# A self-attention residual added in DRAM by accumulating transfers instead of on GpSimd

## The chip, the cores and the metric

The kernel runs on one core of one Trainium2 chip. The metric is the device time of that core in microseconds (us), the median of several executions. Everything is float32.

## The reference, cut to what matters

A transformer block works on eight images of 512 rows and 512 features. A cross-attention with modulated layer norm (phase x), a self-attention (phase a), a second cross-attention (phase c) and an MLP (phase m) follow each other, and each adds its result to x:

```python
x = x_q + (out @ Wp + bp)                  # phase x
attn_out = attn_out @ W_proj + b_proj
x = x + gate_a[:, None] * attn_out         # phase a: the line that the change is about
x = x + c_attn_out                         # phase c
x = x + gate_m[:, None] * h                # phase m
```

`gate_a` is a row of 512 numbers for each image. The softmax of phase a runs over 16 heads of 512 x 512 scores.

## The kernel before, in words

**Where x lies.** x travels through DRAM between the phases. Phase x leaves it in `xa` (one tensor for each image), phase a writes `xc`, and phases c and m read `xc`. Phases x and c already add their results by accumulating transfers: GpSimd (POOL) issues a DMA from the SBUF tile `res` to DRAM with `accum_op=ALU.add` (L665). Such a transfer reads the SBUF source and the DRAM destination and writes the sum back. In phase x, `xa` is filled with a copy of x first (L866). Phase c adds in place to `xc`.

**Phase a, `self_phase`.** The work is cut into 32 groups, four for each image `b`, counted `fc` = 0 to 3; a group is four heads. All engines' orders are written out by hand in one loop over the groups (`manual_schedule(engines=None)`): the order in the source is the order on each engine, and an instruction that waits holds up what follows it on its engine. In the turn of group `g`:

- TensorE (PE) makes the transposed scores of the *next* group, four key tiles of 128 (`nxt.scores(k)`, L991). ScalarE (ACT) copies them to `e` in SBUF (L1009) and VectorE (DVE) keeps a running maximum `mx` (L1011).
- `maxima` and `spread` turn the maxima into one negated number for each query (L1022 to L1035), and SyncE (SP) writes these 8 KB to the DRAM row `mxd` (L1040).
- `shift(k)`, L1045: POOL issues eight accumulating DMAs, two for each key tile, which read `mxd` broadcast over the 128 partitions and add it into the `e` tiles in SBUF, 512 KB each. All eight wait for `mxd` to have landed.
- `exp(k)`, L1054: ACT takes the exponential of each shifted tile. POOL and DVE add the tiles up for the denominators (`add_up`, L1061), and PE multiplies with the values (`outputs`, L1071).

The loop calls `g.exp(0)`, `nxt.scores(3)`, `g.exp(1)`, later `g.exp(2)`, and in the next turn `prev.exp(3)`. So a late shift of key tile 0 holds up ACT's copies of the next group's last scores, and with them the maxima of the next group.

**Beside the attention** each turn runs other products, as generators that `pump` advances: values, queries and keys of the coming image in `fc` 0, 2 and 3, and the output projection of the *previous* image, `project(b - 1, t)`, for `t` = 0 and 1 in `fc` 1 and `t` = 2 and 3 in `fc` 2. In `fc` 2 the next image is transposed (L912) and the one after it is loaded, 1 MB on ACT's queue (`load_x`, L900).

**The residual of phase a.** Four steps for each of the 32 tiles of 128 rows:

- `load_tile`, L906: SP loads the tile's rows of x from `xa` into `xr`, four tiles at a time, at the start of `fc` 0. For the last image the loads stand in the tail behind the loop.
- L960: DVE takes the projection out of PSUM and adds the bias row, into `tmp` (tile `res`).
- `add`, L963 and L964: POOL multiplies `tmp` with the gate row and adds it to `xr`.
- `store`, L967: SP writes `xr` to `xc`.

`add` and `store` are put into two lists and run by `flush(0)` and `flush(1)` at two places of the turn: after the shifts were issued, and before `g.exp(0)`. With this placement one tile's `add` and `store` run in the middle of `fc` 1, one early in `fc` 2, and two in the middle of `fc` 2. For the last image, whose projection stands in the tail, they run tile by tile, and phase c begins behind them.

**Queues.** SP's DMAs run on the queue that the profile calls q1, ACT's on q10, and all of POOL's on q0. As the program is built, POOL's DMAs take eight completion semaphores in turn, so that each waits, at its issue, for the POOL DMA eight places before it.

Of the kernel before, what the change touches and what calls it, by code (L numbers as in the profile page):

```python
# [11 lines left out]
F32 = mybir.dt.float32  # L12
I32 = mybir.dt.int32
AF = mybir.ActivationFunctionType
ALU = mybir.AluOpType
# [4 lines left out]
P = 128  # L20
H = 512
KC = H // P
# [7 lines left out]
def tile_pixart_block(ctx: ExitStack, tc: tile.TileContext, a: dict, out: bass.AP):  # L30
    nc = tc.nc
    x, ctx_in, cond = a["x"], a["ctx_1024"], a["cond_1024"]
    B, N, _ = x.shape
    S = ctx_in.shape[1]
    NT = N // P
# [8 lines left out]
    dram = ctx.enter_context(tc.tile_pool(name="dram", bufs=1, space=bass.MemoryType.DRAM))  # L44
# [40 lines left out]
    def bias_cols(name, n=1, at=0):  # L85
        c = col_at[name] + at
        return bcol[:, c : c + n]
# [33 lines left out]
    def load_context(pool):  # L121
# [11 lines left out]
    x_src = {  # L133
        "x": [x[b] for b in range(B)],
        "a": [dram.tile([N, H], F32, name=f"xa_{b}") for b in range(B)],
        "c": [dram.tile([N, H], F32, name=f"xc_{b}") for b in range(B)],
    }
    x_src["m"] = x_src["c"]
    x_dst = {"x": x_src["a"], "a": x_src["c"], "c": x_src["m"], "m": [out[b] for b in range(B)]}
    x_order = [(ph, b) for ph in "xacm" for b in range(B if ph in "xc" else 1)]  # L140
    x_sb = {}
# [11 lines left out]
    with tc.tile_pool(name="setup_ps", bufs=2, space=PSUM) as spp:  # L153
# [4 lines left out]
        for name, n in col_names:  # L158
            at = col_at[name]
            nc.gpsimd.dma_start(  # L160
                out=brow[at : at + n, :],
                in_=a[name][0 : n * P].rearrange("(c p) -> c p", p=P),
# [149 lines left out]
    def fold_value_bias(name, at, w, row, pool, psp, bufs=2):  # L312


        wide = pool.tile([P, KC, P], F32, tag="res", bufs=bufs, name=f"wide_{name}")
        nc.vector.tensor_copy(wide, bias_cols(name, KC, at).unsqueeze(2).to_broadcast([P, KC, P]))
        ps = psp.tile([P, H], F32, tag="m", name=f"fold_ps_{name}")
        for k in range(KC):
            nc.tensor.matmul(
                ps, lhsT=wide[:, k, :], rhs=w[:, k, :], start=(k == 0), stop=(k == KC - 1)  # L320
            )
        nc.vector.tensor_tensor(row, ps, row, ALU.add)
# [16 lines left out]
    with tc.tile_pool(name="ps_s", bufs=2, space=PSUM, reuse_waits="tile") as ps_s:  # L339
# [539 lines left out]
        def self_phase(w, bo_row, work, work_2, ctx_c):  # L879
# [1 line left out]


            w_v, w_q, w_k, w_o = w
            st = [dict(xT=[], v={}, o=[], q={}, k={}, x={}) for _ in range(B)]
            bias = "L1_xcond_b_qkv"
            SQ = 32
            KQ = N // SQ
# [11 lines left out]
            def load_x(b):  # L899
                nc.scalar.dma_start(  # L900
                    out=x_cur, in_=x_src["a"][b].rearrange("(t p) d -> p t d", p=P)
                )

            def load_tile(b, t, queue=nc.scalar):
                xr = work.tile([P, H], F32, tag="xr", bufs=4, name=f"xr_a{b}_{t}")
                queue.dma_start(out=xr, in_=x_src["a"][b][ts(t, P), :])  # L906
                st[b]["x"][t] = xr

            def transpose_x(b, k):
                pt = ps_m.tile([P, H], F32, tag="m", name=f"lnT_ps_a{b}_{k}")  # L910
# [41 lines left out]
            def project(b, t):  # L952
                if t == 0 and b + 1 < B:
                    st[b]["g"] = gate_rows(gate_a, b, work, "a")
                pr = ps_m.tile([P, H], F32, tag="m", name=f"proj_ps_a{b}_{t}")
                for i, _ in enumerate(mm_N(pr, w_o, st[b]["o"], ts(t, P))):
                    if i == KC - 1:
                        xr = st[b]["x"].pop(t)
                        tmp = work.tile([P, H], F32, tag="res", bufs=3, name=f"res_a{b}_{t}")
                        nc.vector.tensor_tensor(tmp, pr, bo_row, ALU.add)  # L960

                        def add():
                            nc.gpsimd.tensor_tensor(tmp, tmp, st[b]["g"], ALU.mult)  # L963
                            nc.gpsimd.tensor_tensor(xr, xr, tmp, ALU.add)  # L964

                        def store():
                            nc.sync.dma_start(out=x_dst["a"][b][ts(t, P), :], in_=xr)  # L967

                        later[0].append(add)
                        later[1].append(store)  # L970
                    yield
# [142 lines left out]
            for k in range(KC):  # L1114
                transpose_x(0, k)
            load_x(1)
            fold_value_bias(bias, 2 * KC, w_o, bo_row, work, ps_m, 3)
            run(queries(0, 0))
            run(keys(0, 0))
            for k, gen in enumerate([values(0, 0), values(0, 1), queries(0, 1), keys(0, 1)]):  # L1120
# [7 lines left out]
            for n, g in enumerate(groups[:-1]):  # L1128
                b, fc = g.b, g.fc
                nxt = groups[n + 1]  # L1130
                more = b + 1 < B
                f = beside(b, fc)
                turning = fc == 2 and more
                if fc == 3:
                    ln = normalise_x("a", b + 2, True) if b + 2 < B else iter(())
                if not more and fc == 1:
                    ctx_c.w_k = load_w("L1_xcond_W_kvc", 0)
                if prev is not None:
                    prev.outputs(1)
                nxt.scores(0)  # L1140
                g.spread()
                if past is not None:
                    past.total()
                    past.finish()
                if prev is not None:
                    prev.add_up(2, [0])
                g.shift(0)
                if prev is not None:
                    prev.add_up(2, [1])
                    prev.exp(3, [0])  # L1150
                for k in range(1, NT):
                    g.shift(k)
                flush(0)
                flush(1)
                if fc == 0 and b > 0:
                    for t in range(NT):
                        load_tile(b - 1, t, nc.sync)
                if fc == 1 and more:
                    next(ln)
                pump(f[0], 4)  # L1160
                nxt.scores(1)
                if fc == 3 or (b, fc) == (0, 0):
                    next(ln, None)
                    next(ln, None)
                elif fc == 0 and more:
                    next(ln)
                if turning:
                    transpose_x(b + 1, 0)
                if prev is not None:
                    prev.exp(3, [1])  # L1170
                    prev.outputs(2)
                if fc == 1 and more:
                    next(ln)
                pump(f[1], 4)
                if fc == 1 and not more:
                    ctx_c.load()
                    ln = ctx_c.norm()
                if turning:
                    transpose_x(b + 1, 1)
                nxt.scores(2)  # L1180
                if turning:
                    transpose_x(b + 1, 2)
                if fc == 2 and not more:
                    next(ln)
                    next(ln)
                if prev is not None:
                    prev.add_up(3)
                if (b, fc) == (0, 0):
                    next(ln)
                if prev is not None:  # L1190
                    prev.outputs(3)
                if turning:
                    transpose_x(b + 1, 3)
                    if b + 2 < B:
                        load_x(b + 2)
                flush(0)
                flush(1)
                g.exp(0)
                pump(f[2], 2)
                nxt.scores(3)  # L1200
                pump(f[2], 2)
                g.exp(1)
                g.add_up(1)
                if fc == 2 and not more:
                    run(ln)
                nxt.maxima()
                g.outputs(0)
                pump(f[3], 4)
                if fc == 2 and not more:
                    ctx_c.transpose()  # L1210
                g.exp(2)
                past, prev = prev, g
# [29 lines left out]
            for k in range(NT):  # L1242
                g.exp(k)
                if k:
                    g.add_up(k)
                g.outputs(k)
                if k == 0:
                    st[g.b]["g"] = gate_rows(gate_a, g.b, work, "a")
                    for t in range(NT):
                        load_tile(B - 1, t, nc.sync)  # L1250
                if k < len(fills):
                    run(fills[k])
            w_c = [load_w("L1_xcond_W_qc", 0, queue=nc.scalar)]
# [59 lines left out]
        with ExitStack() as stack:  # L1313
            ps_m = stack.enter_context(tc.tile_pool(name="ps_x", bufs=2, space=PSUM, reuse_waits="tile"))
# [17 lines left out]
        with tc.tile_pool(name="work_a", bufs=2, reuse_waits="tile") as work, tc.tile_pool(  # L1332
            name="ps_a", bufs=2, space=PSUM, reuse_waits="tile"
        ) as ps_m, tc.tile_pool(
            name="ps_o", bufs=2, space=PSUM, reuse_waits="tile"
# [5 lines left out]
        with ExitStack() as stack:  # L1341
            ps_m = stack.enter_context(
                tc.tile_pool(name="ps_c", bufs=2, space=PSUM, reuse_waits="tile")
            )
# [21 lines left out]
    bo_row = load_row("L1_xcond_b_mlp2", 0, "bo")  # L1366
    with tc.tile_pool(name="mlp", bufs=1, reuse_waits="tile") as mlp, tc.tile_pool(
        name="mlp_w", bufs=MC // KC - 1, reuse_waits="tile"
    ) as mlp_w, tc.tile_pool(
        name="ps_q", bufs=6, space=PSUM, reuse_waits="tile"  # L1370
    ) as ps_q, tc.tile_pool(
        name="ps_t", bufs=2, space=PSUM, reuse_waits="tile"
# [10 lines left out]
        xT = xpool.tile([P, KC, N], F32, tag="x", name="xT_m")  # L1383
# [253 lines left out]
```

## Time and profile before

| | us |
|---|---|
| median of 3 runs (2554.19 to 2556.33) | 2554.23 |
| the profiled execution, its own time | 2556.85 |
| its span, first to last instruction | 2555.1 |

| engine | busy us | share |
|---|---|---|
| PE | 2437.6 | 95% |
| DVE | 1776.1 | 70% |
| ACT | 1224.9 | 48% |
| POOL | 1103.1 | 43% |

The page cuts the span into 40 slices of 64 us; a digit is the busy share in tenths.

```profile
PE   7999999989999999999988999998999999999998
...
POOL 2245452277776877768663445445102102012011
PEclk9899999999999999999999999999999999999999
DMA  7323323499999899999995213133111011011010
```

Phase a fills the slices from about 460 us to 1370 us. In it PE stands at 9 or 8, and so does the mean of the 16 DMA engines; after it the DMA engines fall to 0 to 5. The clock granted to PE is full almost everywhere.

These are the transfers that the change touches, as the page's last part lists them: destination, source, queue, count, size of one, and the median time from issue to landing.

```profile
e_a<-mxd_a POOLq DMA_DIRECT2D x256, 512.0 KB, 11.7
xa<-res_x POOLq DMA_DIRECT2D x32, 256.0 KB, 5.2
xr_a<-xa SPq DMA_DIRECT2D x32, 256.0 KB, 6.1
xc<-xr_a SPq DMA_DIRECT2D x32, 256.0 KB, 8.6
```

### The profile page before, as it was taken

The page shows a single profiled execution, that of the slowest core. Times are in us where ns is not written, and L with a number is a line of the kernel's source. Part 1 is how long each engine was busy: PE and PEld are TensorE (multiplying, and loading weights), DVE is VectorE, ACT ScalarE, POOL GpSimd, SP SyncE. Part 2 cuts the span into 40 slices and gives each one's busy share as a digit, 9 for nine tenths or more (in the row PEclk, how much of TensorE's full clock was granted, in tenths as well). Part 3 has the DMA queues.
Part 4 walks back from the last instruction along what each step waited for, and adds up shares of the span by engine and source line. Part 5 has one row for each costly group of instructions (what it writes and reads, how often), then busy time and mean ns, then how long its engine had stood idle before and what let it go on. Part 6 is the DMA issues. An engine that isn't in the chain of part 4 may idle for free. (4 is left out here: it accounts for less than half of the span.)

```text
span 2555.1 us, 35387 instructions
## 1 busy us (share of the span) xinstructions
PE 2437.6 (95%) x13205; PEld 1562.6 (61%) x13205; DVE 1776.1 (70%) x3230; ACT 1224.9 (48%) x2083; POOL 1103.1 (43%) x982
## 2 busy tenths in 40 slices
PE   7999999989999999999988999998999999999998
PEld 3577776323333333333325777777888888888887
DVE  3588886478788888887756888887546545555553
ACT  1466665477676776767643666662121121121220
POOL 2245452277776877768663445445102102012011
PEclk9899999999999999999999999999999999999999
DMA  7323323499999899999995213133111011011010
GB/s 259 135 51 95 89 27 74 102 180 193 198 179 205 183 199 195 180 199 180 216 210 171 72 34 67 18 64 98 36 35 38 33 39 38 25 34 49 20 35 25
DMA packets 116676, 273.44 MB, mean 107 GB/s; under 512 B 12722, under 2 KB 29186, under 8 KB 116378
## 3 DMA queue, kind: packets, MB, share of 16 engines
q0 software_dynamic: 46368, 151.06, 33.0%
q1 hardware_dynamic: 64197, 108.37, 12.6%
q10 hardware_dynamic: 5941, 11.76, 1.3%
q8 instruction: 104, 1.70, 0.3%
q14 instruction: 66, 0.54, 0.1%
HBM read 234.78 MB, written 44.76 MB: 109 GB/s over the span
## 5 line engine op out<-in xcount | busy, mean ns | idle before, releaser
L1546 POOL TENSOR_TENSOR res_m<-res_m,gate_m 128x256 f32<-128x256 f32 x64 | 52.1, 814 | 665.1 <-DVE res_m L1544 665.1
L1045 POOL DMA_DIRECT2D e_a<-mxd_a x256 | 250.4, 2060 | 157.9 <-DMA mxd_a<-mxT_a 148.6
L1054 ACT ACTIVATE e_a<-e_a 128x1024 f32<-128x1024 f32 x256 | 265.1, 1058 | 98.4 <-DMA e_a<-mxd_a 98.0
L1009 ACT COPY e_a<-sT_a 128x1024 f32<-128x1024 f32 x256 | 254.2, 1010 | 91.0 <-DVE mx_a L1011 49.0
L1480 ACT ACTIVATE hT<-hT,bcol 128x512 f32<-128x512 f32 x128 | 91.9, 721 | 237.0 <-DVE hT L1455 228.9
L1061 POOL TENSOR_TENSOR sum_a<-e_a,e_a 128x1024 f32<-128x1024 f32 x64 | 150.2, 2363 | 105.8 <-ACT e_a L1054 105.4
L1011 DVE TENSOR_TENSOR mx_a<-sT_a,mx_a 128x1024 f32<-128x1024 f32 x128 | 150.9, 1216 | 33.6 <-PE sT_a L991 27.9
L1061 POOL TENSOR_TENSOR sum_a<-sum_a,e_a 128x1024 f32<-128x1024 f32 x64 | 171.2, 2686 | 5.3 <-ACT e_a L1054 5.3
L991 PE MATMUL sT_a<-qT_a,kT_a 32*128 32x512 f32 x1024 | 151.4, 640 | 17.7 <-ACT e_a L1009 16.1
L1071 PE MATMUL o_ps_a<-e_a,v 128*32 128x512 f32 x1024 | 152.9, 608 | 12.8 <-ACT e_a L1054 12.8
L1447 PE MATMUL q_ps_h<-x_m,w_L_xcond_W_mlp 128*128 128x256 f32 x512 | 132.3, 381 | 0.0
L1447 PE MATMUL q_ps_h<-xT_m,w_L_xcond_W_mlp 128*128 128x256 f32 x512 | 131.6, 380 | 0.0
L294 PE MATMUL q_ps_a<-xnT_a,w_L_xcond_W_qkv 128*128 128x512 f32 x256 | 124.1, 613 | 7.6 <-ACT xnT_a L914 7.6
L1089 DVE RECIPROCAL rz_a<-z_ps_a 128x512 f32<-128x512 f32 x32 | 107.4, 3357 | 31.9 <-PE z_ps_a L1082 31.9
L1447 PE MATMUL q_ps_h<-x_m,w_s 128*128 128x256 f32 x512 | 121.9, 381 | 5.3 <-DVE w_s L1401 4.6
L302 PE MATMUL proj_ps_a<-w_L_xcond_W_proj,oT_a 128*128 128x512 f32 x256 | 118.1, 605 | 3.1 <-DVE res_a L960 1.7
L294 PE MATMUL k_ps_a<-xnT_a,w_L_xcond_W_qkv 128*128 128x512 f32 x256 | 120.5, 608 | 0.0
L302 PE MATMUL v_ps<-w_L_xcond_W_qkv,xnT_a 128*128 128x512 f32 x256 | 119.7, 611 | 0.0
L991 PEld LDWEIGHTS sT_a<-qT_a,kT_a 32*128 32x128 f32 x1024 | 42.4, 183 | 117.7 <-ACT e_a L1009 51.9
L1447 PE MATMUL q_ps_y<-w_L_xcond_W_mlp,h_s 128*128 128x256 f32 x512 | 113.1, 379 | 0.0
L1447 PE MATMUL q_ps_y<-w_L_xcond_W_mlp,hT 128*128 128x256 f32 x512 | 113.1, 379 | 0.0
L1447 PE MATMUL q_ps_y<-w_t,h_s 128*128 128x256 f32 x512 | 111.8, 379 | 0.0
(368 smaller groups left out, 5531.1 us busy)
## 6 DMA issues: line engine op xcount, KB each, us to landing
e_a<-mxd_a POOLq DMA_DIRECT2D x256, 512.0 KB, 11.7
xa<-res_x POOLq DMA_DIRECT2D x32, 256.0 KB, 5.2
xr_a<-xa SPq DMA_DIRECT2D x32, 256.0 KB, 6.1
xc<-xr_a SPq DMA_DIRECT2D x32, 256.0 KB, 8.6
x_c<-xc SPq DMA_DIRECT2D x8, 1024.0 KB, 5.1
w_L_xcond_W_mlp<-in_L_xcond_W_mlp_dram SPq DMA_DIRECT2D x8, 1024.0 KB, 6.9
xc<-res_c POOLq DMA_DIRECT2D x32, 256.0 KB, 5.0
x_m<-xc SPq DMA_DIRECT2D x8, 1024.0 KB, 5.4
```

The costliest lines, as they stand in the source:

```text
L294: nc.tensor.matmul(ps, lhsT=w[:, k, ts(j, P)], rhs=xT[k], start=(k == 0), stop=(k == KC - 1))
L302: nc.tensor.matmul(ps, lhsT=xT[k][:, cols], rhs=w[:, k, :], start=(k == 0), stop=(k == KC - 1))
L991: nc.tensor.matmul(sc[h // 2][:, h % 2, :], lhsT=kT[ts(h, HD), ts(k, P)], rhs=qT[ts(h, HD), :], start=True, stop=True,)
L1009: nc.scalar.copy(self.e[k][i], sc[i])
L1011: nc.vector.tensor_tensor(self.mx[1 - i], sc[1 - i], self.e[0][1 - i] if k == 1 else self.mx[1 - i], ALU.max,)
L1045: nc.gpsimd.dma_start(out=self.e[k][i].rearrange("p h n -> p (h n)"), in_=self.mxd[2 * i : 2 * i + 2, :] .rearrange("h n -> (h n)").partit ...
L1054: nc.scalar.activation(self.e[k][i], self.e[k][i], AF.Exp)
L1061: engine.tensor_tensor(sum_i, self.e[0][i] if k == 1 else sum_i, self.e[k][i], ALU.add)
L1071: nc.tensor.matmul(self.po[ts(h, HD), :], lhsT=vt[:, self.fc * P + h * HD : self.fc * P + (h + 1) * HD], rhs=self.e[k][h // 2][:, h % 2, : ...
L1089: nc.vector.reciprocal(r, self.pz)
L1447: nc.tensor.matmul(self.banks[n][:, half], lhsT=lhsT, rhs=rhs, start=(k == 0), stop=(k == len(pairs) - 1),)
L1480: nc.scalar.activation(dst, src, AF.Gelu_apprx_tanh, bias=bias_cols("L1_xcond_b_mlp1", 1, j))
```

## The change

`xc` is gone: `x_src["c"]`, `x_src["m"]` and all destinations before the output are `xa`. The rows of x are no longer loaded for the residual (`load_tile`, its two calls and the tile `xr` go), POOL's addition L964 goes, and `store` becomes an accumulating DMA that POOL issues from `tmp` into `xa`. The tile `res` gets four buffers instead of three. The places at which `add` and `store` run stay.

```diff
-        "c": [dram.tile([N, H], F32, name=f"xc_{b}") for b in range(B)],
     }
-    x_src["m"] = x_src["c"]
+    x_src["c"] = x_src["m"] = x_src["a"]
...
-            def load_tile(b, t, queue=nc.scalar):
-                xr = work.tile([P, H], F32, tag="xr", bufs=4, name=f"xr_a{b}_{t}")
-                queue.dma_start(out=xr, in_=x_src["a"][b][ts(t, P), :])
-                st[b]["x"][t] = xr
...
-                        xr = st[b]["x"].pop(t)
-                        tmp = work.tile([P, H], F32, tag="res", bufs=3, name=f"res_a{b}_{t}")
+                        tmp = work.tile([P, H], F32, tag="res", bufs=4, name=f"res_a{b}_{t}")
                         nc.vector.tensor_tensor(tmp, pr, bo_row, ALU.add)
 
                         def add():
                             nc.gpsimd.tensor_tensor(tmp, tmp, st[b]["g"], ALU.mult)
-                            nc.gpsimd.tensor_tensor(xr, xr, tmp, ALU.add)
 
                         def store():
-                            nc.sync.dma_start(out=x_dst["a"][b][ts(t, P), :], in_=xr)
+                            nc.gpsimd.dma_start(
+                                out=x_dst["a"][b][ts(t, P), :], in_=tmp, accum_op=ALU.add
+                            )
...
-                if fc == 0 and b > 0:
-                    for t in range(NT):
-                        load_tile(b - 1, t, nc.sync)
...
-                    for t in range(NT):
-                        load_tile(B - 1, t, nc.sync)
```

More of the change, by code (lines that the diff above doesn't have):

```diff
@@ L883, in self_phase @@
             w_v, w_q, w_k, w_o = w
-            st = [dict(xT=[], v={}, o=[], q={}, k={}, x={}) for _ in range(B)]
+            st = [dict(xT=[], v={}, o=[], q={}, k={}) for _ in range(B)]
             bias = "L1_xcond_b_qkv"
@@ L1116, in self_phase @@
             load_x(1)
-            fold_value_bias(bias, 2 * KC, w_o, bo_row, work, ps_m, 3)
+            fold_value_bias(bias, 2 * KC, w_o, bo_row, work, ps_m, 4)
             run(queries(0, 0))
```

## Prediction

> **What bounds the kernel now.** I read the page first, then the table of stretches over the turns of one image, then the timelines of SP, POOL and ACT around the turn that stands out, and last the DMA queues. All times are from the span's start.
>
> The change lies in phase a. There the page shows two kinds of waiting on the path from `mxd` over the shifts to the exponentials (the second number from the left is the mean in ns, the numbers behind the bar are idle time and its cause):
>
> ```profile
> L1045 POOL DMA_DIRECT2D e_a<-mxd_a x256 | 250.4, 2060 | 157.9 <-DMA mxd_a<-mxT_a 148.6
> L1054 ACT ACTIVATE e_a<-e_a 128x1024 f32<-128x1024 f32 x256 | 265.1, 1058 | 98.4 <-DMA e_a<-mxd_a 98.0
> ```
>
> The stretches are cut where DVE ends the maxima (L1035): `fc` 0, 1, 2, 3 of image 3, then `fc` 3 of image 6. Columns: stretch, length, busy time of PE, PE's weight load, DVE, ACT, POOL, clock, DMA share, GB/s.
>
> ```profile
> 800.80:826.50 25.70, 24.37 (x109) 7.83 (x112) 23.19 (x32) 18.04 (x20) 16.39 (x12) 1.00 0.96 207
> 826.50:851.47 24.97, 24.25 (x105) 7.71 (x105) 20.74 (x22) 19.42 (x22) 19.85 (x16) 1.00 0.92 180
> 851.47:879.17 27.70, 26.58 (x125) 9.68 (x129) 21.51 (x22) 19.65 (x22) 23.63 (x19) 1.00 0.95 193
> 879.17:905.67 26.50, 25.89 (x109) 8.08 (x113) 22.23 (x28) 18.23 (x20) 18.20 (x13) 1.00 0.90 183
> 1197.17:1221.64 24.47, 24.28 (x109) 7.82 (x113) 19.07 (x19) 18.08 (x22) 17.06 (x13) 1.00 0.89 173
> ```
>
> PE fills the turns, so PE's work is the floor, but the DMA engines are as full. The same work of `fc` 3 takes 26.50 us here and 24.47 in image 6. Over images 1 to 5 it takes 27.01, 28.05, 26.50, 26.83 and 27.10, which is 13.1 us above five times 24.47. `fc` 0 of images 2 to 6 takes 130.3 us against a floor of 5 x 24.37, 8.5 us above. `fc` 2 stands at 27.7 in every image and `fc` 1 near its floor. So **about 22 us can be won in the turns, and only there**.
>
> Why `fc` 3 is late, on SP, POOL and ACT:
>
> ```profile
> 871.04 5.49 SPq L967 DMA_DIRECT2D xc<-xr_a  x3
> 879.49 26.94 SPq L1040 DMA_DIRECT2D mxd_a<-mxT_a  x2
> ```
> ```profile
> 888.01 1.79 POOL L1045 DMA_DIRECT2D e_a<-mxd_a  x2 [4.86 <-DMA mxd_a<-mxT_a]
> ```
> ```profile
> 893.14 1.06 ACT L1054 ACTIVATE e_a<-e_a 128x1024 f32<-128x1024 f32 x1
> 895.89 1.06 ACT L1054 ACTIVATE e_a<-e_a 128x1024 f32<-128x1024 f32 x1 [1.70 <-DMA e_a<-mxd_a]
> ```
>
> Three residual stores go out on SP, and `mxd` follows on the same queue. POOL's first shift starts 8.5 us after `mxd` was issued (888.01 - 879.49); in the other turns of this image it is 5.8 to 6.0 us. The second exponential waits 1.70 us for its shift, and ACT's next score copies stand behind it.
>
> **The change, part by part.**
>
> *POOL.* Removed: 32 additions L964, median 1.28 us. Added: 32 issues. Their nearest row is phase x's accumulating store:
>
> ```profile
> L665 POOL DMA_DIRECT2D xa<-res_x x32: 869/1062/1208, 151.6 to 454.9; - x32
> ...
> DMA to landing us min/median/max: 3.6/5.2/10.7
> ```
>
> I take 1.04 us (the mean of this row) and 0.16 for the wait on the multiplication (5.0 us of idle over the 32 of phase x). That saves 0.08 us a tile. A rule speaks against it: the Trainium skill, "SBUF — State Buffer" (the "DVE blocks DMA" trap), says that DMAs issued from GpSimd are starved of their descriptors while DVE holds the shared port pair, and gives about 620 ns alone against about 3100 beside such a DVE operation. By the rule the three stores of `fc` 2 cost 3 x 2 = 6 us more than by the row, past the 4.86 us for which POOL stands idle behind them, of which some 2.3 are left once `mxd` comes earlier. The row has no issue over 1208 ns although DVE works beside it, so I take the row and keep 1 us a turn for the range.
>
> Each store also waits for the POOL DMA eight places before it. In `fc` 1 and for the first of `fc` 2 that is the turn's own first shift, landed before its exponential starts at 13.7 us into the turn (840.18 in image 3), where the store comes near 17.6. The others wait for the second and third shift; the third is issued at 9.7 us and, early among the eight, lands sooner than their median of 11.8 us after issue, so before 21.5, about when that store comes. Conversely, the last three shifts of `fc` 3 wait for the three stores. None of these waits bites by my times; behind them on POOL would stand the sums and shifts, and ACT behind those. DVE's L960 has four buffers, so it waits for the store four tiles back, long landed.
>
> *SP.* Removed: 32 loads and 32 stores. Nothing there waited long: `mxd` was issued 0.04 us after the maxima (879.45). What goes is what stood **ahead of `mxd` in the queue**: 8.5 us becomes 5.9 in `fc` 3, and the next wait to end is the shifts' own DMA.
>
> *DMA engines.* The queues' own rows, first for the stretch 700 to 900, second for 260 to 440 (phase x); packets, MB, share of 16 engines:
>
> ```profile
> q0 software_dynamic: 8578, 31.26, 84.0%
> q1 hardware_dynamic: 3094, 4.66, 6.7%
> ```
> ```profile
> q0 software_dynamic: 2304, 4.20, 16.8%
> ```
>
> A shift costs 0.840 x 200 / 31.26 = 5.37 us of all engines per MB, a copy 2.88, an accumulating store in phase x 0.168 x 180 / 4.20 = 7.2. A tile of 0.262 MB thus loses a load and a store (2 x 0.75 = 1.51 us) and gains 1.41 (at the shifts' rate) to 1.89 us (phase x's). I take 1.65. Per image that is 0.6 us more, in all 4 us; the DMA work of an image goes from some 98 to 98.5 us of 105. The sum hardly moves; its place does.
>
> In `fc` 0 four loads, 3.0 us of engine time, no longer cut into the last shifts of `fc` 3 and the first of `fc` 0. I take 0.7 of the 1.7 us that this turn stands above its floor: 7 images, **-5 us**. Ends: 0 and -1.7 each.
>
> In `fc` 2 and 3 a second rule decides. The Trainium skill, "DMA: Bandwidth & Descriptors" (Queues, rings and completion order), says that a DMA engine serves the queues it has work for in turn, packet by packet. Before, the stores on q1 thus ran between the shifts; on q0 they run whole, after the shifts of `fc` 2 and **ahead of those of `fc` 3**. By the row of `mxd` alone I would write 2.6 us for each turn, -16 us for six. By the rule: the last shift of `fc` 2 landed at 887.4 (its exponential starts there), and without the stores' 3 x 0.75 between them at 885.1. Three stores of 1.65 keep q0 until 890.1. The first shift, issued near 885.4, lands one shift's time (0.524 MB x 5.37 = 2.8) later, at 892.9; the second at 895.7, the third at 898.5, the fourth at 901.3. Before, their exponentials started at 893.1, 895.9, 899.7 and 902.2. So the first two win 0.2 us and the later ones about 1. I take 0.8 us for images 1 to 6: **-5 us**. Ends: stores of 1.41 win 1.5 us a turn, stores of 1.89 lose 0.5.
>
> *The tail.* Four POOL steps as before in length. New: as built, ACT's first `xnT` copy of phase c (1368.33) waits for the first of the four last stores, because it takes over that memory. The store is issued near 1362.2 and lands 5.2 us later, at 1367.4; by the row's ends -0 to +4.6 us. PE and all of phase c stand behind it. I take **+1**. Phases x, c and m keep their transfers, under another name.
>
> **Sum:** -5 - 5 + 1, and POOL's 0: -9 us; with 4 us of added DMA work, of which I charge 1, -8. Against the execution's own 2556.9 (1.8 more than its span) that is 2548.9; its span would be 2547.1. The median lies 2.6 us below the profiled execution, so 2554.2 - 8 = **2546**.
>
> **Rivals.**
>
> *The floors are reached* (chance 0.11). Both turns fall to PE's time: -22 us, 2532. For it: POOL and ACT have room in every turn. Against it: the DMA engines keep 98 of 105 us.
>
> *Nothing comes of it* (0.20), 2554: the DMA work is the same, `fc` 3 waits for its shifts as before and `fc` 0 had another cause. For it: the second exponential moves by 0.2 us only. That the stores were not what delayed `mxd` would end here too.
>
> *The store in front of the shifts costs* (0.26): one mechanism, in q0 between `fc` 2 and `fc` 3. It decides from the point where the second shift lands later than 895.9: (895.9 - 5.6 - 885.1) / 3 = 1.73 us a store, hardly above what I took and below phase x's 1.89. At 2.6 us, if beside saturated engines a store takes half again as much as mine, the second shift lands 2.7 us late in six turns, +16, less the 5 of `fc` 0: 2565. For it: landings of up to 10.7 us in phase x. Against it: shifts keep their rate in the fullest stretches.
>
> *My forecast* (0.43) has its own range of 2537 to 2552.
>
> **Range and chances.** 2534 to 2564 reaches nearly to the floors below and to the third rival's price above. No change is within 0.2% (5 us), about what a measurement of this kernel can tell. Faster, under 2549: 0.11 and 0.39 of the forecast, 0.50. Same: 0.20 and 0.04, 0.24. Slower: 0.26.
>
> **What would show it.** In the changed profile the first shift of `fc` 3 starts about 6 us after `mxd` (5.5 to 6.5), its second exponential at 16.5 us into the turn or earlier, `fc` 3 shortens to about 26 and `fc` 0 to about 25.3 us, and the queue's cost per MB stays under 5.6. Wrong would be: POOL issues of over 2 us for the stores, waits of POOL before them, landings above 12 us with `fc` 3 at 28 us, or a copy of `xnT` that waits for a store for more than 3 us.

## The result and the profile after

| | before | after |
|---|---|---|
| median, us | 2555.28 (4 runs, 2554.19 to 2558.96) | 2540.03 (4 runs, 2538.55 to 2543.09) |
| profiled execution, own time | 2556.85 | 2543.09 |
| its span | 2555.1 | 2541.3 |

The change makes the kernel 15.2 us faster, a ratio of 0.9943 (95% interval 0.993 to 0.9957). The forecast was 2546, 8 us under before, with a range of 2534 to 2564.

The groups of the page, with the same columns as before the change (mean ns second, idle time and its cause behind the bar):

```profile
L1039 POOL DMA_DIRECT2D e_a<-mxd_a x256 | 250.0, 2048 | 162.5 <-DMA mxd_a<-mxT_a 154.0
...
L1048 ACT ACTIVATE e_a<-e_a 128x1024 f32<-128x1024 f32 x256 | 265.0, 1058 | 68.2 <-DMA e_a<-mxd_a 67.6
```

ACT's wait for shifts fell from 98.0 to 67.6 us. POOL's wait for `mxd` did not fall: it starts to wait earlier now. The turns tell more. The stretches again: `fc` 0, 1, 2, 3 of image 3, then `fc` 3 of image 6.

```profile
797.31:822.97 25.66, 24.37 (x109) 7.83 (x112) 23.15 (x32) 18.20 (x21) 16.54 (x13) 1.00 0.89 168
822.97:848.34 25.37, 25.25 (x109) 7.95 (x112) 20.57 (x22) 19.68 (x22) 19.52 (x15) 1.00 0.92 176
848.34:875.80 27.46, 26.48 (x125) 9.56 (x128) 21.53 (x21) 20.36 (x24) 23.33 (x19) 1.00 0.96 190
875.80:900.27 24.47, 24.28 (x109) 7.82 (x112) 22.14 (x27) 17.60 (x20) 16.21 (x12) 1.00 1.07 204
1186.31:1210.78 24.47, 24.28 (x109) 7.81 (x112) 19.07 (x19) 17.39 (x20) 16.25 (x12) 1.00 0.96 176
```

The fourth line is the one to look at: `fc` 3 has gone from 26.50 to 24.47 us, the same as in image 6, where it was at its floor from the start. `fc` 0, the first line, is unchanged (25.70 before). The timelines of that `fc` 3 on SP, POOL and ACT:

```profile
876.11 0.45 SPq L1034 DMA_DIRECT2D mxd_a<-mxT_a  x1
```
```profile
882.60 0.89 POOL L1039 DMA_DIRECT2D e_a<-mxd_a  x1 [4.61 <-DMA mxd_a<-mxT_a]
```
```profile
889.48 1.06 ACT L1048 ACTIVATE e_a<-e_a 128x1024 f32<-128x1024 f32 x1
890.74 1.06 ACT L1048 ACTIVATE e_a<-e_a 128x1024 f32<-128x1024 f32 x1 [0.21 <-DMA e_a<-mxd_a]
```

The first shift starts 6.5 us after `mxd` (8.5 before). The second exponential starts 14.9 us into the turn (16.7 before) and waits 0.21 us for its shift instead of 1.70. Over images 1 to 5, `fc` 3 takes 122.7 us in place of 135.5.

The profiled executions differ by 13.8 us of span. Phase a ends 9.1 us earlier (its last projection at 1358.8, before 1367.9), with -12.8 in these five turns and losses in others, the largest in `fc` 1 of image 0 (+3.1) and `fc` 0 of image 7 (+3.8). Much of that belongs to the single execution: in c1_after_again below, the same kernel, these two turns lose 0.4 and 1.8 us, and the last projection ends at 1352.1. Phases c and m keep their lengths to within 0.8 us. The last 3.9 us lie behind all arithmetic, in POOL's closing DRAIN. Here are its rows, before and then after; minimum, median and maximum in ns:

```profile
L1633 POOLq DRAIN  x3: 51/98/7617, 2546.7 to 2554.8; - x3
```
```profile
L1622 POOLq DRAIN  x3: 46/98/3743, 2536.8 to 2541.0; - x3
```

### The profile page after: what moved, and what is told of

It is laid out like the page before. It is cut to its first block, busy times and chain, and to the rows that moved or that the text cites. A ratio compares the mean times of both kernels' runs of the same rounds, so it can differ in the third digit from the quotient of the medians.

```text
span 2541.3 us, 35276 instructions
## 1 busy us (share of the span) xinstructions
PE 2432.2 (96%) x13205; PEld 1560.3 (61%) x13205; DVE 1779.8 (70%) x3230; ACT 1228.0 (48%) x2083; POOL 1085.5 (43%) x982
## 3 DMA queue, kind: packets, MB, share of 16 engines
q0 software_dynamic: 50976, 159.45, 34.9%
## 4 chain that ended last, share of the span: by engine, by line
PE 41%; issue 28%; DVE 15%; DMA 7%; POOL 6%; ACT 3%; POOLq 0%; SPq 0%; ACTq 0%; DVEq 0%
PE s_ps_qx L509 4%; PE s_ps_qc L509 4%; DMA e_a<-mxd_a 3%; DVE mx_a L1005 3%; PE proj_ps_a L301 3%; PE sT_a L985 3%; PE v_ps L301 3%; PE s_ps_ox L509 2%; PE s_ps_oc L509 2%; DVE tu_a L1016 2%; POOL res_m L1535 2%; PE q_ps_a L293 2%; DVE part_a L1017 2%; PE o_ps_a L1065 2%; POOL xr L1536 2%
## 5 line engine op out<-in xcount | busy, mean ns | idle before, releaser
L1048 ACT ACTIVATE e_a<-e_a 128x1024 f32<-128x1024 f32 x256 | 265.0, 1058 | 68.2 <-DMA e_a<-mxd_a 67.6
L1005 DVE TENSOR_TENSOR mx_a<-sT_a,mx_a 128x1024 f32<-128x1024 f32 x128 | 150.9, 1218 | 28.1 <-PE sT_a L985 25.8
L1065 PE MATMUL o_ps_a<-e_a,v 128*32 128x512 f32 x1024 | 148.5, 609 | 12.1 <-ACT e_a L1048 11.9
L1451 ACT COPY p_h<-q_ps_h 128x256 f32<-128x256 f32 x64 | 23.7, 370 | 183.7 <-PE q_ps_h L1436 183.7
## 6 DMA issues: line engine op xcount, KB each, us to landing
e_a<-mxd_a POOLq DMA_DIRECT2D x256, 512.0 KB, 11.6
xa<-res_a POOLq DMA_DIRECT2D x32, 256.0 KB, 15.2
```

Of the source, the lines that this page charges most:

```text
L1005: nc.vector.tensor_tensor(self.mx[1 - i], sc[1 - i], self.e[0][1 - i] if k == 1 else self.mx[1 - i], ALU.max,)
L1048: nc.scalar.activation(self.e[k][i], self.e[k][i], AF.Exp)
L1065: nc.tensor.matmul(self.po[ts(h, HD), :], lhsT=vt[:, self.fc * P + h * HD : self.fc * P + (h + 1) * HD], rhs=self.e[k][h // 2][:, h % 2, : ...
```

## The experiments

Three theories stood against each other first. The **queue theory**: the gain comes from the stores that no longer stand ahead of `mxd` on q1. The **load theory** and the **addition theory**: it comes from the loads of `fc` 0 or from POOL's additions. The table gives, from each profile, the mean turn of `fc` 3 (images 1 to 5) and of `fc` 0 (images 2 to 6), cut as above, and when the first shift of `fc` 3 starts.

| kernel | median us | ratio to before (95%) | `fc` 3 | its first shift at | `fc` 0 |
|---|---|---|---|---|---|
| before | 2555.28 | | 27.1 | 8.7 to 9.6 | 26.1 |
| after | 2540.03 | 0.9943 (0.993 to 0.9957) | 24.5 | 5.8 to 7.1 | 26.0 |
| c1_after_again | 2540.64 | 0.9945 (0.9932 to 0.9958) | 24.5 | 5.8 to 6.9 | 26.0 |
| e1_store_pool | 2542.88 | 0.9954 (0.9942 to 0.9966) | 24.8 | 6.0 to 7.1 | 25.8 |
| e2_store_behind_mxd | 2543.49 | 0.9951 (0.9939 to 0.9964) | 24.8 | 6.3 to 7.5 | 26.1 |
| e12_half_pool | 2541.72 | 0.9944 (0.9932 to 0.9956) | 25.0 | 6.1 to 7.6 | 26.0 |
| e3_loads_back | 2540.76 | 0.9946 (0.9934 to 0.9958) | 24.9 | 5.8 to 7.3 | 25.9 |
| e4_no_loads | 2554.74 | 0.9998 (0.999 to 1.0006) | 27.1 | 8.1 to 9.6 | 26.0 |
| e5_add_back | 2544.74 | 0.9965 (0.9953 to 0.9977) | 25.7 | 6.3 to 6.9 | 25.6 |
| e6_acc_behind_shifts | 2539.90 | 0.9941 (0.9927 to 0.9955) | 24.5 | 5.8 to 6.9 | 26.2 |
| e7_fc0_sum_later | 2559.19 | 1.0017 (1.0011 to 1.0024) | 24.5 | 5.7 to 6.6 | 28.2 |
| e9_fc0_sum_behind_third | 2569.54 | 1.005 (1.0036 to 1.0063) | 24.6 | 5.8 to 6.8 | 30.4 |
| e11_fc0_sum_dve | 2534.62 | 0.9928 (0.9916 to 0.994) | 24.6 | 6.2 to 7.2 | 25.2 |

Before ran beside each group of kernels, with medians of 2554.4 to 2555.3.

### The stores: which engine, which place

e1, on the kernel before:

```diff
-                            nc.sync.dma_start(out=x_dst["a"][b][ts(t, P), :], in_=xr)
+                            nc.gpsimd.dma_start(out=x_dst["a"][b][ts(t, P), :], in_=xr)
```

> The kernel before, with its store L967 issued by POOL instead of SP; it stays a plain copy of xr into xc, and the loads and POOL's addition stay. The queue theory (the gain is that the stores no longer stand on q1 ahead of mxd and between the last shifts of fc 2): fc 3 of images 1 to 5 falls from 27.1 us to under 25, its first shift starts less than 7.5 us into the turn, and the time is 9 to 15 us under before. The load theory (the gain comes from the loads of fc 0 that are gone) and the addition theory (from POOL's additions that are gone): fc 3 stays at 26.5 to 28 us and the time within 3 us of before.

`fc` 3 falls to 24.8 us with loads and additions still there, and the time by 11.5 us. So neither is needed for the gain. But e1 changes the queue as well as the place. e2 changes the place alone:

```diff
                 flush(0)
-                flush(1)
+                if fc != 2:
+                    flush(1)
                 g.exp(0)
```

> The kernel before, with only the place of two stores moved: in fc 2 the stores of the last two tiles are issued on SP behind the next turn's mxd instead of ahead of it. Queue, loads and POOL's addition stay. If the order in the queue is the cause: the first shift of fc 3 starts less than 7.5 us into the turn (before 8.7 to 9.6), fc 3 falls from 27.1 to between 24.5 and 25.5 us, and the time is 7 to 13 us under before. If it is the stores' sharing of the DMA engines with the shifts, wherever they stand: fc 3 stays above 26 us and the time within 4 us of before.

The store lists then wait for the next turn's `flush(1)`, which stands behind `spread`. SP's timeline of e2 at the start of `fc` 3 of image 3, and POOL's first shift there:

```profile
874.66 0.45 SPq L1040 DMA_DIRECT2D mxd_a<-mxT_a  x1
875.20 1.07 SPq L967 DMA_DIRECT2D xc<-xr_a  x2
```
```profile
881.75 1.79 POOL L1045 DMA_DIRECT2D e_a<-mxd_a  x2 [3.41 <-DMA mxd_a<-mxT_a]
```

The same bytes go over the same queue, now half a microsecond behind `mxd` instead of ahead of it, and `mxd` reaches POOL after 7.1 us instead of 8.5. The time falls by 11.6 us. **What costs is the order on q1**: 8 KB that all of a turn waits for, behind stores of 256 KB for which nobody waits. The DMA packets in the traces say the same for `fc` 3 of images 1 to 5: the first packet of `mxd` starts 5.3 to 6.6 us after its issue before, and 3.5 to 4.0 us after it in e2 and in the changed kernel, although in e2 packets of the stores still run until 6.7 to 7.8 us after that issue. That the stores share the DMA engines with the shifts can thus not be the whole cost. That it is no part of it is not shown: counted from the issue of `mxd`, the last shift of `fc` 2 also lands 1.3 to 3.1 us earlier in e2.

e12 issues by POOL only the stores of tiles 2 and 3, which are the two that come last in `fc` 2:

```diff
-                            nc.sync.dma_start(out=x_dst["a"][b][ts(t, P), :], in_=xr)
+                            queue = nc.sync if t < 2 else nc.gpsimd
+                            queue.dma_start(out=x_dst["a"][b][ts(t, P), :], in_=xr)
```

> The kernel before, with only every second pair of stores, tiles 2 and 3 of each image, issued by POOL as plain copies (16 of the 32). The order theory: none of the two stores of fc 2 that come last stands ahead of mxd any more, so fc 3 falls to 24.4 to 25 us as in e1_store_pool, and the time by 9 to 14 us. For the end of the kernel: if POOL's last DRAIN grows or shrinks with the number of DMAs that POOL has issued, it lies between that of before (7.6 us) and of e1_store_pool (3.2 us), near 5.4; if it has two values only, it is one of them.

12.9 us faster: these two stores carry the effect. (Its end is taken up below.)

### The loads and the addition

e3 puts the loads back into the changed kernel (with `res` at three buffers again; the rows come from the input `x`, the same number of bytes), e4 takes them out of the one before. Of e3, the loads:

```diff
+                if fc == 0 and b > 0:
+                    for t in range(NT):
+                        xr = work.tile([P, H], F32, tag="xr", bufs=4, name=f"xr_a{b - 1}_{t}")
+                        nc.sync.dma_start(out=xr, in_=x[b - 1][ts(t, P), :])
```

> The changed kernel, with the four loads of 256 KB for each image put back at the start of fc 0, on SP, into tiles that nothing reads (the tile res has three buffers again, for room). The load theory: fc 0 and fc 3 lengthen by about 1 us each and the time rises by 5 to 12 us. The queue theory, and the trace of the change, in which fc 0 did not get shorter without the loads: within 3 us of the changed kernel.

> The kernel before without the 32 loads L906 (POOL's second operation then adds the gated projection to itself, so that x is missing from the output); stores on SP and POOL's work stay. The prediction's step for the loads: fc 0 of images 2 to 6 falls from 26.1 to 25.4 us or less, and the time by 4 to 8 us. The theory from the runs so far, that fc 0 waits for DVE and the loads cost nothing: fc 0 stays at 25.7 to 26.2 us, fc 3 at 26.5 to 28 us, and the time within 3 us of before.

Both agree: 0.7 us and -0.3 us. The loads cost nothing that can be measured, and `fc` 0 keeps its 26 us with and without them. e5 adds a POOL operation to the changed kernel:

```diff
                             nc.gpsimd.tensor_tensor(tmp, tmp, st[b]["g"], ALU.mult)
+                            nc.gpsimd.tensor_tensor(tmp, tmp, st[b]["g"], ALU.add)
```

> The changed kernel with a second POOL operation of 128 x 512 for each tile behind the multiplication, as the addition of before was (it adds the gate row once more, so the output differs by that). The addition theory: fc 3 goes back to 26 us or more and the time rises by 6 to 13 us. The queue theory: POOL has room in every turn of fc 1 and 2, the four steps of the tail cost 1.3 us each at most, and the time rises by 0 to 5 us.

4.4 us over the mean of the two medians of after (2540.3), inside what the queue theory allowed, but for another reason than it gave: POOL does not have room. ACT's timeline of e5 at the boundary of `fc` 2 and 3 of image 3:

```profile
873.35 1.01 ACT L1004 COPY e_a<-sT_a 128x1024 f32<-128x1024 f32 x1 [2.13 <-POOL sum_a L1056]
875.64 1.01 ACT L1004 COPY e_a<-sT_a 128x1024 f32<-128x1024 f32 x1 [1.28 <-POOL sum_a L1056]
```

The next scores can't be copied until POOL's sums release `e`; in the changed kernel ACT makes the corresponding two copies at 875.99 with no wait at all. `fc` 3 stands at 25.7 us in each image. A further 2.8 us are lost in the tail: POOL's products `sq_c`, for which phase c's queries wait, stand behind the residual's last steps, and the first scores of phase c start 16.1 us after the last projection instead of 13.2. So the addition that went matters after all: it makes room for the accumulating issue (0.89 us each, against 0.58 for the plain issue of e1, which keeps the addition and has `fc` 3 at 24.8). By itself it doesn't make the gain, since e2 has it too.

### The rival: stores in front of the shifts

e6 makes the same edit as e2, on the changed kernel.

> The changed kernel with the last two stores of fc 2 issued behind the eight shifts of fc 3 instead of ahead of them in the same queue. The prediction's rival, that the stores in q0 hold up the shifts of fc 3: the first shift lands 2 to 3 us earlier. As fc 3 is at its floor already, the time stays within 3 us of the changed kernel; if the stores then stand in the way of fc 0 (first shift over 7.5 us into the turn), it is 3 to 8 us longer.

The time is that of the changed kernel, and the first shift of `fc` 3 lands 10.7 to 11.9 us into the turn in images 1 to 5, against 11.1 to 12.5. The stores in front of the shifts delay them by 0.6 us in the mean and 1.4 at most, not by 2 to 3, and at no cost that can be measured.

### What `fc` 0 waits for

If not for the loads, why does `fc` 0 stand at 26 us over a floor of 24.4? DVE's timeline of the changed kernel in `fc` 0 of image 4, then POOL's:

```profile
908.37 2.76 DVE L220 TENSOR_SCALAR lnv_a<-mv_a 128x4 f32<-128x4 f32 x1
911.16 0.17 DVE L222 TENSOR_SCALAR lny_a<-lnv_a 128x4 int32<-128x4 int32 x1
```
```profile
908.07 3.02 POOL L1055 TENSOR_TENSOR sum_a<-sum_a,e_a 128x1024 f32<-128x1024 f32 x1
```

An operation on four numbers a partition takes 2.76 us and ends 0.04 us after POOL's sum. DVE's maxima, ACT's copies and the exponentials (15.3 us into the turn, 13.7 in a turn at its floor) stand behind it. It was to be read before, in the row of this operation (min/median/max in ns):

```profile
L221 DVE TENSOR_SCALAR lnv_a<-mv_a x8: 158/2338/3145, 384.7 to 1125.2; 128x4 f32<-128x4 f32 x8
```

e7 moves the sum behind the second pair of shifts, e9 behind the third:

```diff
                 if prev is not None:
-                    prev.add_up(2, [1])
+                    if fc:
+                        prev.add_up(2, [1])
                     prev.exp(3, [0])
                 for k in range(1, NT):
                     g.shift(k)
+                    if prev is not None and not fc and k == 1:
+                        prev.add_up(2, [1])
```

> The changed kernel with one POOL sum of fc 0 (the second half of add_up(2), L1055) put behind the second pair of shifts, so that it no longer runs beside DVE's L220. The theory for fc 0: L220, 0.16 us in the other phases, takes 2.5 us here because it waits for POOL's sum; DVE's maxima and ACT's copies then come late, and fc 0 stands 1.5 us above its floor for that and not for the loads. By it L220 falls to about 0.2 us, fc 0 of images 1 to 6 falls from 25.9 to between 24.4 and 25 us, and the time by 4 to 9 us. If the 2.5 us are L220's own or are made by POOL's DMA issues, L220 stays above 1.5 us and the time within 2 us of the changed kernel.

> As e7_fc0_sum_later, but the sum of fc 0 stands behind the third pair of shifts instead of the second. In e7 the wait moved from L220 to L225, two operations on, which ended with POOL's sum (920.66 and 920.62). If DVE's small tensor_scalar operations cannot run while POOL's sum runs or is about to: with 1.8 us more of shifts ahead of the sum all three are through before it, L220 and L225 take 0.2 to 0.3 us, fc 0 of images 1 to 6 falls from 25.9 to between 24.4 and 25 us, and the time is 4 to 9 us under the changed kernel. If one of them waits again, fc 0 is 27 us or more.

Both are slower than before, by 0.17 and 0.5%, and both say why. In e7 the wait stays on L220 in five of the six images, with 3.7 to 4.4 us, and is on L225 in the sixth, which is image 4 (4.5 us). DVE and POOL of e9 in image 4:

```profile
923.88 5.51 DVE L228 TENSOR_TENSOR lnt_a<-lnt_a,lnv_a 128x4 f32<-128x4 f32 x1
```
```profile
924.93 4.42 POOL L1055 TENSOR_TENSOR sum_a<-sum_a,e_a 128x1024 f32<-128x1024 f32 x1
```

Here, in image 4, all three `tensor_scalar` are through in 0.18 us each or less, as foreseen, and then a `tensor_tensor` waits 5.5 us until POOL's sum ends (929.35). The victim changes, the release doesn't. It is told by the Trainium skill, "SBUF — State Buffer" (Who interferes with whom): a DVE operation with two inputs in SBUF, or in a two-port mode, and a GpSimd operation that reads SBUF exclude each other, and the second waits until the first ends. The runs agree that the wait ends with POOL's sum. Whether L220 runs in a two-port mode no run here shows. And in e9 it isn't seen that the sum came first: DVE's operation is held from 923.88 on, 1.05 us before the trace has the sum start, while POOL still issues shifts. So the wait is longer than POOL's operation (2.36 us alone); why it begins so early stays open. The remedy then is not to shift the sum but to take it away from POOL:

```diff
-                    prev.add_up(2, [1])
+                    prev.add_up(2, [1], dve=fc == 0)
```
```diff
-                    engine = nc.vector if k == NT - 1 else nc.gpsimd
+                    engine = nc.vector if dve or k == NT - 1 else nc.gpsimd
```

> The changed kernel with the second half of the third sum of fc 0, add_up(2, [1]), on DVE instead of POOL, in front of DVE's maxima. If in fc 0 DVE's small operations wait for POOL's sum: no POOL sum stands beside them any more, L220 to L242 take 0.16 to 0.3 us each, DVE pays 1.2 us for the sum in place of a wait of 2.6 us, fc 0 of images 1 to 6 falls from 25.9 to 24.4 to 25.2 us, and the time is 4 to 9 us under the changed kernel. If fc 0 is bound by DVE's work as such: fc 0 stays at 25.5 to 27 us and the time within 3 us of the changed kernel or over it.

```profile
L220 DVE TENSOR_SCALAR lnv_a<-mv_a x8: 159/160/206, 385.9 to 1114.0; 128x4 f32<-128x4 f32 x8
```

That row is e11's: 160 ns in the median instead of 2501. In image 4 these small operations of DVE run while POOL issues its eight shifts (904.6 to 911.8), so the issues alone do not hold DVE. `fc` 0 of images 1 to 6 takes 150.5 us instead of 155.2, about half of what it stood above its floor (6 x 24.37 = 146.2); what the other half waits for stays open. `fc` 1 gives 1.7 of the gain back. The median of 2534.62 is 6.0 us under that of c1_after_again beside it, and the fastest of all kernels here; the two intervals against before still overlap, and e11's profiled execution (2539.74) is not faster than c1's (2535.73). So the size of the step is less sure than its cause.

### The end of the kernel

> The changed kernel unaltered, beside the two that follow. If the short end (POOL's last DRAIN lasts 3.2 to 3.8 us in every kernel whose stores POOL issues, 7.6 us in the three whose stores SP issues) belongs to the kernel: 3.7 us again, and the time 2537 to 2544 us. If it varies by chance from execution to execution: anything between 3 and 8 us.

It is 3.74 us again. The closing DRAIN belongs to the kernel, to within 0.01 us wherever the packets are the same, but it follows no simple count:

| kernels | packets of q0 | POOL's closing DRAIN, us |
|---|---|---|
| before, e2, e4 | 46368 | 7.62 |
| e12 | 47648 | 2.11 |
| e1 | 48928 | 3.17 |
| after, c1, e3, e5, e6, e7, e9, e11 | 50976 | 3.74 |

e12 was to lie between before and e1, or to equal one of them; it lies below both. The DRAIN changes with what went through POOL's queue more than a millisecond earlier; how it does so stays open. Filling that queue with other transfers of the same number of packets was not tried.

## Why the prediction was right, and where it was not

**The sum** was right in sign and half in size: -8 against -15.2. That it came so near is in part luck: `fc` 0 was put 4.5 us too high and `fc` 3 7.8 us too low, and the end of the kernel was not in it.

**SP and `mxd`: right.** The step "8.5 us becomes 5.9 in `fc` 3" measured 6.5 in image 3, and e2 shows that the order on q1 alone is worth 11.6 us.

**`fc` 3, "-5 us": right in mechanism, too small.** It measured -12.8. The step that failed is the chain of landings that ended with the second shift at 895.7, 16.5 us into the turn. It came at 14.9. The last shift of `fc` 2 landed where it was put (33.8 us into its turn, against 33.6), but the three stores took 3.7 us together, not 4.95 (they land at 34.9, 36.2 and 37.5), and the two shifts 2.4 and 2.5 us, not 2.8 each. That is 1.25 and 0.7 us less; the last shift's 0.2 and a turn of `fc` 2 shorter by 0.2 take 0.4 back, and 16.5 becomes 15.0. Both sizes came from the queue's busy share for each MB. That share counts packets which overlap (it reads 1.07 in the stretch of `fc` 3 above) and overstates the interval between landings, which the trace of before showed as 2.5 us for successive shifts of this `fc` 3 (beside the stores and the load of 1 MB in `fc` 2 they landed 2.6 to 4.0 us apart). With the second shift at 14.9 nothing holds the turn above its floor, so the first rival was right for this half of its claim. The queue's cost, 0.919 x 200 / 34.50 = 5.33 us for each MB, stayed under the 5.6 named:

```profile
q0 software_dynamic: 10037, 34.50, 91.9%
```

**`fc` 0, "-5 us": wrong.** It measured -0.5 in images 2 to 6. The step that failed is "I take 0.7 of the 1.7 us that this turn stands above its floor": that excess was put down to the loads because they stood there, not because anything waited for them. e3 and e4 show that it did not belong to the loads, and e11 that about half of it belonged to DVE's wait for POOL. The seventh image, which the step counted too, has its `fc` 0 at 29.0 us in the changed kernel and 27.0 in c1, against 25.2 before; why was not followed up.

**POOL, "0.08 us a tile": too little credit for the addition, and rightly no penalty for the issue.** The rows of the store:

```profile
L959 POOL DMA_DIRECT2D xa<-res_a x32: 859/891/1448, 632.6 to 1361.2; - x32
...
  POOL res_a L956: 5.1, 17
...
DMA to landing us min/median/max: 3.9/15.2/17.6
```

In the changed kernel no issue came near the 3100 ns of the rule that the prediction weighed; the row of phase x was the better guide. (In e6, where two stores follow eight shifts at once, an issue takes 2.9 to 3.6 us. But the issues of shifts grow in the same way one by one, from 0.9 to 3.3 us over eight in a row in `fc` 3 of image 3 of before, so that is no sign of the rule.) The stores land late (15.2 us), behind the shifts in q0, and nobody waits for them. So of the sign "landings above 12 us with `fc` 3 at 28 us" the first half came true and the second did not. What the 0.08 left out is the price if the room on POOL is gone: with one more operation a tile, as in e5, ACT's copies and phase c wait for POOL and 4.4 us are lost.

**The tail, "+1", and "4 us of added DMA work, of which I charge 1": both nothing.** The first copy of `xnT_c` waits for PE and starts at 1359.3, just behind the last projection, with no store in its way.

**Not in the prediction:** the 3.9 us of the closing DRAIN, a quarter of the gain. The order on q1 (11.6 by e2, whose DRAIN is still 7.62) and this end together make 15.5, which is the measured change within its interval. That the two simply add is not shown: by the same account e1, whose end is 4.4 us shorter, should have won 16 and won 11.5, and e12, whose end is 5.5 us shorter, should have won 17 and won 12.9. Of e1's missing 4.5 its `fc` 3 (0.3 us over the changed kernel's, five times) and the first scores of phase c, 14.9 us after the last projection instead of 13.3, account for 3; the rest is of the size of the spread between executions.

**The rivals.** "The store in front of the shifts costs" was to decide at 1.73 us a store; a store took 1.3, and e6 closes the case. "Nothing comes of it" fell with `fc` 3. "The floors are reached" held for `fc` 3 and not for `fc` 0.

## What to carry to other kernels

Look at what stands ahead of a small transfer on the critical path in its own queue: moving two bulky, unwaited stores behind it won 11.6 us, where rebuilding the residual won 15.2. For how long a queue holds the next transfer, take the spacing of landings in that stretch of the trace, not the busy share for each MB. And before an excess is put down to whatever happens nearby, look for an operation whose median in that place is many times its median elsewhere.

## What the runs showed of the hardware that was not expected

- A DVE operation of 0.16 us waits for a POOL sum of 2.36 us until that ends, and for longer (up to 5.6 us in e9) when POOL still issues DMAs ahead of the sum.
- POOL's closing DRAIN lasts 2.1 to 7.6 us. It is the same to 0.01 us in kernels with the same packets on POOL's queue, and differs with transfers that lie more than a millisecond back.
- An accumulating store of 256 KB into DRAM, queued behind shifts, lands 1.3 us after the one before it; its issue takes 0.89 us in the median, that of a plain one 0.58.
